# One denominator product for eight attention units inside the v projection, its rows folded by transfers

## Chip, cores, metric

One core of one Trainium2 chip. The metric is the device time of one execution in microseconds (us), as the median of several runs. Engines: PE is TensorE, DVE is VectorE, ACT is ScalarE, POOL is GpSimd, SP issues most DMAs. The kernel's tiles lie in SBUF, in up to 128 partitions; PE writes its products to PSUM tiles, from which ACT and DVE read them (for q: PE writes pq, ACT reads it as 128x512 and DVE as 128x1024). A record is one matmul in the trace.

## The reference, cut to what matters

Eight images of 512 channels by 1024 positions go through an attention block with eight heads, then a nonlocal block with a batch norm over all images.

```python
q = _conv1x1(x, Wq, bq).reshape(B, h, d, H * W)          # B 8, h 8, d 64, H*W 1024
k = _conv1x1(x, Wk, bk).reshape(B, h, d, H * W)
v = _conv1x1(x, Wv, bv).reshape(B, h, d, H * W)
attn = jax.nn.softmax(jnp.einsum('bhdn,bhdm->bhnm', q, k) * scale, axis=-1)
out = jnp.einsum('bhnm,bhdm->bhdn', attn, v).reshape(B, C, H, W)
return x + _conv1x1(out, Wp, bp)
```

The kernel sums the exponentials of each softmax row apart from the weighted sum, and multiplies o by the reciprocals of these denominators afterwards. That is all this change touches.

## The kernel before

The attention of an image is done in eight units (four pairs of heads, two halves of the queries). A unit's sums of exponentials end in `acc`, 128 partitions of 1024 columns. Four transfers turn each quarter of its partitions into 32 partitions of `fold`, so that four units fill one `fold` tile (a group), which three adds reduce to 128 x 1024. A matmul with a block matrix of ones (`folds`) sums each unit's 32 partitions: the denominators.

```python
def fold_parts(g, t, pin):
    return [lambda to=to, l=l, r=r: pin(nc.vector.tensor_tensor(to, l, r, ALU.add)) for to, l, r in (
        (t[:, 0], t[:, 0], t[:, 1]), (t[:, 2], t[:, 2], t[:, 3]), (folded[g][:, 0], t[:, 0], t[:, 2]))]

def denominators(g, ps):
    t = folded.pop(g)
    columns(ps, folds, lambda j: t[:, 0, j * 512:(j + 1) * 512])   # two matmuls, 64 columns each
    ...
    nc.vector.reciprocal(ri, ps)
    ...                                                            # ri goes to DRAM as den_d
    return d
# rows_of: two transfers a group spread den_d over 64 partitions each (r); normalize: o = o * r
```

In every image but the last, the first group is folded within the attention, the second in between the matmuls of the next image's q (`fills`). Both products stand between q and v:

```python
q, peak_q = heads_of(b + 1, "q", ..., fills=last_fold)
load_w(nc.sync)
d = [denominators(g, next_bank(f"den_{b}_{g}")[:, 0, :]) for g in range(2)]
v = values(b + 1, weights("WvT"), nxt["data"], {5: normalize(d)})   # products behind v's sixth chunk
```

The kernel uses PSUM as four tags of two banks each. A stage takes its tags from the list `free` in the order in which the stage before leaves them, and `next_bank` takes the tag that comes first and moves it to the end. A projection has up to seven chunks of matmuls, and each chunk's result is read from PSUM by ACT or DVE. `dve(...)` pins an instruction: it keeps its place in DVE's queue as written, where others are placed by a scheduler.

## Time and profile before

| | before |
|---|---|
| median of six runs | 2166.07 us (2164.36 to 2166.74) |
| span in the profile | 2164.2 us |
| PE busy | 2137.3 us, 99% of the span |
| DVE busy | 1427.6 us, 66% |
| waits of PE over 0.15 us | five, 5.6 us in all |

Read it from PE: its busy share and its few waits say that time is to be had only from matmuls that fall away and from those waits. The lines are in the prediction.

### The profile page before, as it was taken

Reading aid. Unit: us, or ns where it says so; the run is one execution under the profiler, and the core shown is the slowest. Engines: PE = TensorE matmul, PEld = TensorE weight load, DVE = VectorE, ACT = ScalarE, POOL = GpSimd, SP = SyncE. Lnnn points to the kernel's source line nnn. Section 1 sums busy time; section 2 is a strip of 40 time slices with the busy share of each in tenths; the row PEclk is TensorE's granted clock in tenths of the full one; section 3 lists DMA queues with packets and bytes.
Section 4 is the critical chain, followed back from the end, with each engine's and each line's share of the span. In section 5 each row is a group of like instructions: output and inputs, shape, how many; then the busy total and the mean of one; then the engine's idle time right before and its main releaser. Section 6 shows DMA issues by size and latency. Waiting matters only on the chain.

```text
span 2164.2 us, 29633 instructions
## 1 busy us (share of the span) xinstructions
PE 2137.3 (99%) x12454; PEld 1110.0 (51%) x12454; DVE 1427.6 (66%) x1612; ACT 740.9 (34%) x848; POOL 43.2 (2%) x50
## 2 busy tenths in 40 slices
PE   9999999999999999999999999999999999999996
PEld 4534664346733567335663366633665346643362
DVE  5477756776477764777747767477773776657736
ACT  1464104631046310563105621066212651056115
POOL 0000100000000000000000000000000000000000
PEclk9999999999999999999999999999999999999998
DMA  6312433123131232312323132231334114111748
GB/s 216 131 36 54 132 151 131 40 62 115 69 132 40 62 115 72 132 38 77 98 102 108 40 89 101 79 108 40 97 135 153 30 40 122 63 53 41 245 150 357
DMA packets 50701, 219.47 MB, mean 101 GB/s; under 512 B 9216, under 2 KB 15616, under 8 KB 43008
## 3 DMA queue, kind: packets, MB, share of 16 engines
q1 hardware_dynamic: 49072, 216.18, 31.2%
q8 instruction: 100, 1.64, 0.3%
q10 hardware_dynamic: 1488, 1.32, 0.2%
q14 instruction: 41, 0.34, 0.0%
HBM read 138.03 MB, written 45.88 MB: 85 GB/s over the span
## 4 chain that ended last, share of the span: by engine, by line
PE 98%; DVE 1%; ACT 1%; DMA 0%; issue 0%
PE ps L422 20%; PE po L448 20%; PE pv L274 9%; PE ptp L274 9%; PE pp L274 7%; PE pk L274 7%; PE pq L274 6%; PE pg L274 4%; PE pf L571 3%; PE pz L274 2%; PE pk_in_s L237 2%; PE pq_in_s L237 2%; PE pp_in_s L237 2%; PE pz L682 2%; PE pwf L606 1%; PE den L394 1%
## 5 line engine op out<-in xcount | busy, mean ns | idle before, releaser
L425 ACT ACTIVATE e<-ps 128x1024 f32<-128x1024 f32 x512 | 522.4, 1024 | 428.3 <-PE ps L422 422.1
L431 DVE TENSOR_TENSOR acc<-acc,e 128x1024 f32<-128x1024 f32 x384 | 470.0, 1224 | 127.7 <-ACT e L425 120.1
L448 PE MATMUL po<-e,v 64*64 64x512 f32 x4096 | 528.7, 589 | 0.7 <-ACT w_WgT L573 0.7
L422 PE MATMUL ps<-q,k 64*64 64x512 f32 x4096 | 529.1, 589 | 0.0
L448 PEld LDWEIGHTS po<-e,v 64*64 64x64 f32 x4096 | 156.5, 133 | 283.4 <-issue 275.4
L422 PEld LDWEIGHTS ps<-q,k 64*64 64x64 f32 x4096 | 155.6, 133 | 284.1 <-issue 275.0
L594 ACT ACTIVATE g<-pg,gb 128x512 f32<-128x512 f32 x31 | 21.3, 687 | 388.6 <-PE pg L274 385.7
L429 DVE TENSOR_TENSOR acc<-e,e 128x1024 f32<-128x1024 f32 x64 | 78.2, 1223 | 108.7 <-ACT e L425 73.4
L274 PE MATMUL ptp<-w_tp,t_x 128*128 128x256 f32 x512 | 115.0, 380 | 0.0
L274 PE MATMUL pv<-w_WvT,t_x 128*128 128x256 f32 x512 | 114.5, 379 | 0.0
L274 PEld LDWEIGHTS pv<-w_WvT,t_x 128*128 128x128 f32 x512 | 97.2, 190 | 13.2
L274 PEld LDWEIGHTS ptp<-w_tp,t_x 128*128 128x128 f32 x512 | 96.7, 190 | 12.9
L274 PE MATMUL pp<-t_o,w_WpT 128*128 128x512 f32 x208 | 100.8, 592 | 0.0
L274 PE MATMUL pq<-t_x,w_WqT 128*128 128x512 f32 x200 | 98.8, 593 | 0.7 <-DVE w_WqT L734 0.7
L274 PE MATMUL pk<-t_x,w_WkT 128*128 128x512 f32 x200 | 98.9, 592 | 0.0
L377 ACT COPY v<-pv 128x1024 f32<-128x1024 f32 x32 | 32.4, 1012 | 191.2 <-PE pv L274 191.2
L274 PE MATMUL pv<-w_WvT,x 128*128 128x256 f32 x384 | 87.5, 381 | 0.0
L274 PE MATMUL ptp<-w_tp,x 128*128 128x256 f32 x384 | 86.8, 379 | 0.0
L378 DVE TENSOR_TENSOR v<-v,pv 128x1024 f32<-128x1024 f32 x24 | 29.3, 1221 | 79.9 <-PE pv L274 79.9
L274 PEld LDWEIGHTS pv<-w_WvT,x 128*128 128x128 f32 x384 | 72.4, 190 | 15.7 <-issue 5.9
L274 PEld LDWEIGHTS ptp<-w_tp,x 128*128 128x128 f32 x384 | 73.0, 190 | 13.3 <-issue 3.6
L478 DVE TENSOR_TENSOR fold<-fold 128x1024 f32<-128x1024 f32 x48 | 58.7, 1222 | 26.0 <-DMA fold<-acc 25.5
(182 smaller groups left out, 2211.3 us busy)
## 6 DMA issues: line engine op xcount, KB each, us to landing
fold<-acc SPq DMA_DIRECT2D x254, 128.0 KB
r<-den_d SPq DMA_DIRECT2D x32, 512.0 KB
x<-in_x_dram SPq DMA_DIRECT2D x31, 512.0 KB
w_WqT<-kept_WqT SPq DMA_DIRECT2D x7, 2176.0 KB
w_WkT<-kept_WkT SPq DMA_DIRECT2D x7, 2176.0 KB
w_WpT<-kept_WpT SPq DMA_DIRECT2D x6, 2176.0 KB
w_WvT<-kept_WvT SPq DMA_DIRECT2D x7, 1792.0 KB
w_tp<-kept_tp SPq DMA_DIRECT2D x7, 1792.0 KB
```

What stands on the lines that cost most here:

```text
L237: pe(nc.tensor.matmul(ps, a[wi], d[di], start=s not in begun, stop=True, skip_group_check=True))
L274: pe(nc.tensor.matmul(to_ps, lhsT(k), rhs(k), start=(s, at) not in begun, stop=(k == nk - 1), skip_group_check=True))
L377: seven(f"pv_{b}", w, data, True, lambda q, ps: nc.scalar.copy(at(q), as_v(ps)), lambda q, ps: dve(nc.vector.tensor_tensor(at(q), at(q), a ...
L378: lambda q, ps: dve(nc.vector.tensor_tensor(at(q), at(q), as_v(ps), ALU.add)), between)
L422: pe(nc.tensor.matmul(ps[c * P // 2:(c + 1) * P // 2, j, :], k[r, p, keys], q[r, p, h * 512:(h + 1) * 512], start=True, stop=True, skip_gr ...
L425: nc.scalar.activation(e, ps, AF.Exp, scale=SCALE)
L429: nc.vector.tensor_tensor(accs[u], es[u, 0], e, ALU.add)
L431: ins = nc.vector.tensor_tensor(accs[u], accs[u], e, ALU.add)
L448: pe(nc.tensor.matmul(ps[j * D:(j + 1) * D, r, :], v[keys, m, (2 * p + j) * D:(2 * p + j + 1) * D], e[keys, j, :], start=(m == 0), stop=(m ...
L478: return [lambda to=to, l=l, r=r: pin(nc.vector.tensor_tensor(to, l, r, ALU.add)) for to, l, r in ((t[:, 0], t[:, 0], t[:, 1]), (t[:, 2], ...
L571: pe(nc.tensor.matmul(ps[:, c, :], tp[:, i, c * P:(c + 1) * P], tp[:, i, CI:], start=(i == 0), stop=(i == NB - 1)))
L682: pe(nc.tensor.matmul(ps[:, h - h0, :], wf[:, d, oc * P:(oc + 1) * P], g[d][:, h * 512:(h + 1) * 512], start=(d == 0), stop=(d == IC - 1), ...
```

## The change

Its intent: one product for all eight units of an image, so that PE does half the denominator work and DVE one reciprocal fewer. To put eight units on 128 partitions, each group's 32 rows per unit are folded to 16: two transfers per group bring the even rows to one place and the odd rows to another, and one more add sums them. The product moves behind v's first chunk, to give the transfers time. Apart from that, the last image's first reading of p is pinned behind the products of o with the rows.

```diff
-                    if done in (6, 8, 10) and fills:
-                        fills[done // 2 - 3]()
+                    if done in fills:
+                        fills[done]()
...
+        def fold_last():
+            t = folded.pop(1)
+            folded["all"] = t[:, 1]
+            adds = [lambda to=to, l=l, r=r: dve(nc.vector.tensor_tensor(to, l, r, ALU.add)) for to, l, r in (
+                (t[:, 0], t[:, 0], t[:, 1]), (t[:, 2], t[:, 2], t[:, 3]), (t[:, 0], t[:, 0], t[:, 2]),
+                (t[:, 1], t[:, 1], t[:, 3]))]
+            first = folded.pop(0)[:, 0]
+            def rows_of(g, half):
+                nc.sync.dma_start(t[g * D:(g + 1) * D, 1 + 2 * half, :],
+                                  (t[:, 0] if g else first).rearrange("(r s) n -> s r n", s=2)[half])
+            return {6: lambda: (adds[0](), rows_of(0, 0)), 8: lambda: (adds[1](), rows_of(0, 1)),
+                    10: lambda: (adds[2](), rows_of(1, 0), rows_of(1, 1)), 14: adds[3]}
...
+        def all_denominators(ps):
+            t = folded.pop("all")
+            columns(ps, folds8, lambda j: t[:, j * 512:(j + 1) * 512])
+            ...
...
+                if b == B - 1 and q == "11":
+                    dve(ins)
...
-            d = [denominators(g, next_bank(f"den_{b}_{g}")[:, 0, :]) for g in range(2)]
-            v = values(b + 1, weights("WvT"), nxt["data"], {5: normalize(d)})
+            def norm():
+                nxt["products"] = normalize(denominators(next_bank(f"den_{b}")[:, 0, :]))
+            v = values(b + 1, weights("WvT"), nxt["data"], {0: norm, 5: lambda: nxt["products"]()})
```

Cut: the building of `folds8` on POOL, the sharing of one tile by `warm` and `heads`, and the shape of `den_d`. The last image keeps two products.

More of the change, by code (lines that the diff above doesn't have):

```diff
@@ L300, in unshifted @@
     xt = xp.tile([P, CC, N], F32, tag="x", name="x_0")
-    warm = const.tile([P, P], F32, tag="warm", name="warm")
-    nc.vector.memset(warm, 0.0)
+    heads = const.tile([P, P], F32, tag="heads", name="heads")
+    nc.vector.memset(heads, 0.0)
     _, w_first = weights_tile("WqT", C // 2)
@@ L315, in unshifted @@
     for i in range(WARM):
-        pe(nc.tensor.matmul(ps[:, :P], warm, warm, start=True, stop=True))
+        pe(nc.tensor.matmul(ps[:, :P], heads, heads, start=True, stop=True))
     bq, bk = load_col("bq", nc.scalar), load_col("bk", nc.scalar)
@@ L328, in unshifted @@
         nc.vector.memset(folds[i * P // 4:(i + 1) * P // 4, i * D // 4:(i + 1) * D // 4], 1.0)
-    heads = const.tile([P, P], F32, tag="heads", name="heads")
-    nc.vector.memset(heads, 0.0)
+    folds8 = const.tile([P, D], F32, tag="folds8", name="folds8")
+    nc.gpsimd.memset(folds8, 0.0)
+    nc.gpsimd.affine_select(out=folds8, in_=folds8, compare_op=ALU.is_gt, fill=1.0, base=1 - P // 8,
+                            pattern=[[-P // 8, 8], [0, D // 8]], channel_multiplier=1)
+    nc.gpsimd.affine_select(out=folds8, in_=folds8, compare_op=ALU.is_ge, fill=0.0, base=0,
+                            pattern=[[-P // 8, 8], [0, D // 8]], channel_multiplier=1)
     for j in range(2):
@@ L479, in fold_parts @@
                 (t[:, 0], t[:, 0], t[:, 1]), (t[:, 2], t[:, 2], t[:, 3]), (folded[g][:, 0], t[:, 0], t[:, 2]))]
+        def all_denominators(ps):
+            t = folded.pop("all")
+            columns(ps, folds8, lambda j: t[:, j * 512:(j + 1) * 512])
+            ri = t[:, :512]
+            nc.vector.reciprocal(ri, ps)
+            d = dram2.tile([16, 512], F32, tag="den", name=f"den_d_{b}")
+            nc.sync.dma_start(d, ri.rearrange("(a s) n -> a s n", a=16)[:, 0, :])
+            d = d.rearrange("(j g i) n -> g j (i n)", j=2, g=2)
+            return d[0], d[1]
         def denominators(g, ps):
@@ L491, in denominators @@
             nc.sync.dma_start(d, ri.rearrange("(a s) n -> a s n", a=8)[:, 0, :])
-            return d
+            return d.rearrange("(j i) n -> j (i n)", j=2)
         def rows_of(g, d):
@@ L498, in rows_of @@
             for j in range(2):
-                sp(nc.sync.dma_start(rows[g][j * D:(j + 1) * D, :],
-                                     d.rearrange("(j i) n -> j (i n)", j=2)[j].partition_broadcast(D)))
+                sp(nc.sync.dma_start(rows[g][j * D:(j + 1) * D, :], d[j].partition_broadcast(D)))
         def normalize(d):
@@ L530, in attention @@
             return o["o"], lambda ps: denominators(1, ps), lambda d: normalize((first_den, d)), None
-        return o["o"], denominators, normalize, fold_parts(1, folded[1], dve)
+        return o["o"], all_denominators, normalize, fold_last()
     def project(b, xt, o, w, between, data=None):
@@ L539, in first @@
                 at = xt[:, c, cols(q)]
-                nc.vector.scalar_tensor_tensor(at, ps[:, m, :], bp[:, c:c + 1], at, ALU.add, ALU.add)
+                ins = nc.vector.scalar_tensor_tensor(at, ps[:, m, :], bp[:, c:c + 1], at, ALU.add, ALU.add)
+                if b == B - 1 and q == "11":
+                    dve(ins)
         seven(f"pp_{b}", w, data or data_sums(quarters_of(o), f"o_{b}"), False, first, add_to(xt), between,
```

## The prediction

> **What bounds the kernel now.** I read the page first, the totals and the chain that ended last:
>
> ```profile
> PE 2137.3 (99%) x12454; PEld 1110.0 (51%) x12454; DVE 1427.6 (66%) x1612; ACT 740.9 (34%) x848; POOL 43.2 (2%) x50
> ...
> PE 98%; DVE 1%; ACT 1%; DMA 0%; issue 0%
> ```
>
> TensorE (PE) is busy 99% of the span and makes 98% of the chain, so the time falls only by matmuls that are not issued, or by PE's idle time. How much idle time there is to win, the waits of PE alone tell:
>
> ```profile
> PE pp L274 <- DVE o L513: 2.6, 1, 2.6
> PE warm_ps L316 <- DVE warm L302: 1.1, 1, 1.1
> PE pq L274 <- DVE w_WqT L734: 0.7, 1, 0.7
> PE po L448 <- ACT w_WgT L573: 0.7, 1, 0.7
> PE den L394 <- PE pg L274: 0.5, 1, 0.5
> ```
>
> Five waits, 5.6 us, only one of them large. Work taken from VectorE (DVE, 66% busy) or from the DMA queues is worth nothing by itself.
>
> Next, the timeline of PE where image 3 hands over to image 4 (other images repeat it), the place of the denominators:
>
> ```profile
> 1007.99 1.88 PE L274 MATMUL pq<-t_x,w_WqT 128*128 128x512 f32 x4
> 1009.80 1.94 PE L394 MATMUL den<-fold,folds 128*64 128x512 f32 x8
> 1011.67 3.72 PE L274 MATMUL pv<-w_WvT,x 128*128 128x256 f32 x16
> ```
>
> Two groups of denominators (four units each) stand one after the other between q and v. PE gives them 1011.67 - 1009.80 = 1.87 us. In the last image a group stands alone, in the timeline there:
>
> ```profile
> 1977.46 1.08 PE L394 MATMUL den<-fold,folds 128*64 128x512 f32 x4
> 1978.47 1.09 PE L422 MATMUL ps<-q,k 64*64 64x512 f32 x8
> ```
>
> One group costs 1978.47 - 1977.46 = 1.01 us, so the second of two costs 1.87 - 1.01 = 0.86 us. (The source issues two matmuls a group and the trace shows four records: each f32 product counts as two.)
>
> What DVE does at that hand-over (its timeline, image 3):
>
> ```profile
> 1005.95 1.21 DVE L296 TENSOR_TENSOR q<-q,pq 128x1024 f32<-128x1024 f32 x1
> 1007.08 0.41 DVE L296 TENSOR_TENSOR q<-q,pq_in_s 128x256 f32<-128x256 f32 x1
> 1007.41 2.34 DVE L363 TENSOR_REDUCE peak_q<-q 128x1 f32<-128x1024 f32 x2
> 1009.91 2.35 DVE L296 TENSOR_TENSOR q<-q,pq 128x1024 f32<-128x1024 f32 x2 [0.16 <-PE pq L274]
> 1012.18 3.35 DVE L487 RECIPROCAL fold<-den 128x512 f32<-128x512 f32 x1
> ```
>
> From 1005.6 to 1021 DVE has no idle time over 0.2 us: q's last partial sums are read from PSUM at 1009.91 to 1012.26, and 3.35 us reciprocals follow.
>
> Last, the one large wait, in the timeline of the last image:
>
> ```profile
> 2025.15 1.10 SPq L499 DMA_DIRECT2D r<-den_d  x2
> 2025.19 2.36 DVE L513 TENSOR_TENSOR o<-o,r 128x1024 f32<-128x1024 f32 x2 [0.90 <-DMA r<-den_d]
> ...
> 2030.27 3.60 PE L274 MATMUL pp<-o,w_WpT 128*128 128x512 f32 x8
> 2033.90 1.41 DVE L540 SCALAR_TENSOR_TENSOR x<-pp,bp,x 128x512 f32<-128x512 f32 x2 [5.09 <-PE pp L274]
> 2035.23 2.35 DVE L513 TENSOR_TENSOR o<-o,r 128x1024 f32<-128x1024 f32 x2
> 2036.50 5.40 PE L274 MATMUL pp<-o,w_WpT 128*128 128x512 f32 x8 [2.63 <-DVE o L513]
> ```
>
> DVE idles 5.09 us, reads the first products of p, and only then multiplies the second half of o by the reciprocals' rows, for which PE waits 2.63 us. DVE is a queue in order, and the reading, which waits for PE, stands ahead of the products.
>
> [...] the last image's first two rows transfers were issued at 2018.25 in bars of 1.11 us together, and the product that needs them waited until 2025.19, 6.94 us after. So when data is there must be read from the waiters.
>
> **The change, part by part** (images 0 to 6 are ordinary; the last keeps its own way, two separate groups).
>
> (a) One product for eight units. Per ordinary image it removes one group of den on PE (0.86 us, on the path: PE never stops there), one reciprocal (3.35 us of DVE) and one write of den to DRAM. It adds four transfers of 256 KB and one add of 1.22 us. On PE: 7 x 0.86 = 6.0 us. On DVE: 7 x (3.35 - 1.22) = 15 us fewer, worth nothing in time.
>
> (b) The product moves from before v to after v's first chunk. A chunk of v is 16 records, 3.45 us by the starts of chunks. The folding has to be done by then. In image 3 the three adds of the second group end at about 1002.2; the transfers of its rows start there. Four transfers of 128 KB from acc to fold in the last image fed their first add 3.4 us after the first issue (issued 2009.41, add at 2012.82); 512 KB again here, so I estimate landing at 1006 to 1007. The closing add stands behind the adds at 1007.08, starts at about 1007.5 and ends at 1008.7. PE comes to den at 1009.80 + 3.45 = 1013.25. So the transfers are hidden.
>
> But the same 1.22 us pushes what DVE does next: peak_q ends at 1011.0 instead of 1009.75, q's last two sums at about 1013.3 instead of 1012.26. By the rotation of PSUM banks in the source, the new den takes the very bank that q's last chunk used (the spare one of v), so it must wait for those sums: 1013.3 plus a tenth for the signal, against 1013.25. I charge 0.1 us an image, 0.7 us in all.
>
> After den: its reciprocal ends by 1019 (with a peak_q of 2.28 ahead of it), the write and the rows follow, issued at about 1021, where before it was 1023 (second reciprocal ended 1021.0). Rows in use start at the product behind v's sixth chunk, some 1 us earlier than now. They are as early as before or earlier: no new wait.
>
> (c) The pinned first reading of the last p. The second pair of rows was issued at 2025.15; with the same 6.94 us as the first pair they are there at 2032.1. The two products then run 2032.1 to 2034.5, the one PE needs first ends at 2033.3, before PE has finished p's first chunk (about 2033.87, 2.63 us before 2036.50). PE's wait of 2.63 us goes whole. The reading starts at 2034.5 instead of 2033.9; its bank is used again two chunks after the next, near 2040.7, so nothing waits for it. The end follows: behind this point PE has no wait over 0.15 us to its last matmul at 2143.5, and the outputs, written at the pace of DMA from the first finished channel group on, start earlier by the same amount.
>
> (d) warm becomes heads, and folds8 is built on GpSimd at the start: heads' ones wait for the warm-up matmuls, which end near 4.9 us, while DVE's next work comes at 8.27. Nothing.
>
> Sum: -6.0 - 2.6 + 0.7 = -7.9 us; 2166.1 - 7.9 = 2158.2, so I say **2158**.
>
> **The rivals.** First, the bank: q's last sums come later than I think (the add waits for the rows' transfers, or the scheduler puts the second peak_q, 2.28 us, ahead of them), and den holds PE each time. For it: DVE is packed there, and the margin is nil. Against it: the sums are pinned in order and ready at 1009.9. At 1 us an image it costs 7 us: some 2164. Second, the rows come too late for the products and DVE, in order, holds v's sums and p or k: for it, four transfers of 512 KB take about 2.4 us each; against it, DVE loses a whole reciprocal ahead of them. With 0.5 us an image: 2161. Third, no bank wait at all: -8.6 us, 2157.4. Fourth, (c) gains little, because the second pair of rows shares the DMA engines with the weights and spills issued behind it and lands after 2033.9: then 2159 to 2160.
>
> **Range and chances.** Runs of the kernel before lie within 2.3 us. The third rival sets the near edge, with that scatter 2155; the others, partly, the far one, 2162. 2% is 43 us: nothing here reaches it either way.
>
> **What would show it.** Right: den has 36 records instead of 64, standing behind the first 16 records of pv; reciprocals 9 instead of 16; from q's last to k's first matmul 0.86 us less in every ordinary image; the wait of pp for o gone and no idle time of DVE between rows and reading; a new entry "den waits for DVE q" of a tenth of a us, seven times. Wrong: that entry at half a us or more, a wait of DVE's o for r in ordinary images with PE gaps behind it in pv or pk, adds of fold waiting for transfers, or pp still waiting.

## The result, and the profile after

| | before | after |
|---|---|---|
| median of six runs | 2166.07 us | 2172.98 us (2169.47 to 2174.78) |
| span in the profile | 2164.2 us | 2173.1 us |

The ratio is 1.0031, 95% interval 1.0018 to 1.0044. (Ratios are the mean time of one kernel's fast runs over that of the other's in the same rounds, so not quite the ratio of the medians quoted.) The change cost 6.9 us where 7.9 us of gain were predicted. It stays within 2%, but outside the range.

The page of the kernel after, busy times and chain:

```profile
PE 2135.7 (98%) x12426; PEld 1110.9 (51%) x12426; DVE 1412.5 (65%) x1611; ACT 741.5 (34%) x848; POOL 44.0 (2%) x53
...
PE 97%; issue 1%; DVE 1%; ACT 1%; DMA 0%
```

The 28 records (7 images x 4) are gone, and DVE has 15 us less to do, as reckoned. But PE's busy time fell by 1.6 us only, and "issue", time for which no releaser is found, is now 1% of the chain. The waits of PE in the kernel after (columns: total us, times, longest):

```profile
PE den L398 <- issue: 13.4, 7, 2.0
PE warm_ps L316 <- DVE heads L302: 1.1, 1, 1.1
PE po L452 <- ACT w_WgT L605: 0.7, 1, 0.7
PE den L398 <- PE pg L274: 0.4, 1, 0.4
```

The wait of pp for o is gone. In its place PE waits before each of the seven new products, up to 2.0 us. The profile names no releaser: PE's sequencer, not DVE or a DMA, stands as the last thing seen. What happens there is shown by the timeline of the hand-over, image 3 of the kernel after (PE, DVE and ACT together; starts are 6.94 us later than in the kernel before, by the last four records of q, 1014.93 against 1007.99):

```profile
1014.93 1.88 PE L274 MATMUL pq<-t_x,w_WqT 128*128 128x512 f32 x4
...
1016.07 1.23 DVE L485 TENSOR_TENSOR fold<-fold 128x1024 f32<-128x1024 f32 x1 [1.64 <-DMA fold<-fold]
1016.64 3.62 PE L274 MATMUL pv<-w_WvT,x 128*128 128x256 f32 x16
...
1017.21 2.34 DVE L367 TENSOR_REDUCE peak_q<-q 128x1 f32<-128x1024 f32 x2
1019.46 2.34 DVE L296 TENSOR_TENSOR q<-q,pq 128x1024 f32<-128x1024 f32 x2
...
1021.91 1.08 PE L398 MATMUL den<-fold,folds 128*64 128x512 f32 x4 [1.65 <-issue]
1022.92 1.35 PE L274 MATMUL pv<-w_WvT,t_x 128*128 128x256 f32 x5
```

Follow DVE down: it idles 1.64 us until the rows have been transferred, adds them, reduces peak_q, and only then reads q's last sums from PSUM, until 1021.80. PE has done v's first chunk at 1020.26, waits 1.65 us, and starts den 0.1 us after q's sums have been read. DVE's wait and PE's wait have the same length, and over the seven images too: DVE waits 13.3 us for these transfers, PE 13.4 us for den. The closing add itself was done at 1017.3. So it is not den's input that holds it.

There is a second loss. The granted clock of PE in three stretches around image 6's den (columns: stretch, us, busy us and count of PE, PEld, DVE, ACT, POOL, then PE's clock, DMA share, GB/s):

```profile
1806.90:1808.90 2.00, 0.01 (x2) 0.04 (x2) 1.97 (x3) 1.00 (x1) 0.00 (x0) 1.00 1.07 453
1808.90:1812.80 3.90, 3.90 (x10) 2.24 (x11) 3.90 (x3) 0.00 (x0) 0.00 (x0) 0.57 0.35 147
1812.80:1816.00 3.20, 3.20 (x16) 2.81 (x16) 1.63 (x1) 0.70 (x1) 0.00 (x0) 0.99 0.04 10
```

PE stands still for 2 us, then runs 3.9 us at a mean clock of 0.57. The records of the clock hold three windows of 3.41 us at 0.5 within the work: after the waits of 1.99, 2.04 and 2.04 us (images 0, 1, 6), none after those of 1.65 to 1.95 us. Each costs 3.41 / 2 = 1.7 us: in image 0 the 32 records of pv behind den take 8.83 us, in image 4, without a window, 7.17 us.

The windows begin at 218.83, 488.48 and 1809.44, 0.55 to 0.98 us after den has started, so the half clock falls on the matmuls behind the wait. Why 1.99 us brought one and 1.95 us did not, these runs do not settle.

The last image, where the pinning acts (timeline of the kernel after):

```profile
2038.43 1.10 SPq L530 DMA_DIRECT2D r<-den_d  x2
2038.47 2.36 DVE L543 TENSOR_TENSOR o<-o,r 128x1024 f32<-128x1024 f32 x2 [1.31 <-DMA r<-den_d]
...
2043.13 7.29 PE L274 MATMUL pp<-o,w_WpT 128*128 128x512 f32 x16
2045.44 2.36 DVE L543 TENSOR_TENSOR o<-o,r 128x1024 f32<-128x1024 f32 x2 [3.35 <-DMA r<-den_d]
```

The second pair of products now starts when its rows land, 7.01 us after their issue (6.94 was assumed), and pp runs through. In the kernel before, the wait of 2.63 us was followed by a half-clock window too (3.41 us from 2036.64 on): eight records of pp took 5.40 us there, and 16 take 7.29 us here.

Adding up by the profiles, from one hand-over to the next: images with no window lose 0.85 to 1.16 us (image 2 to 3: 266.33 against 265.31), those with one 2.85 to 2.90 us (image 0 to 1: 269.87 against 267.02). Together +12.8 us. From the last image's second den to PE's last matmul: 122.01 us against 126.34, -4.3 us. With 0.3 us at the two ends of the program that makes the 8.8 us between the spans (the profiled run was the slowest of the six).

### The profile page after: what moved, and what is told of

Its sections match the earlier page's. It is cut to its first block, busy times and chain, and to the rows that moved or that the text cites.

```text
span 2173.1 us, 29636 instructions
## 1 busy us (share of the span) xinstructions
PE 2135.7 (98%) x12426; PEld 1110.9 (51%) x12426; DVE 1412.5 (65%) x1611; ACT 741.5 (34%) x848; POOL 44.0 (2%) x53
## 4 chain that ended last, share of the span: by engine, by line
PE 97%; issue 1%; DVE 1%; ACT 1%; DMA 0%
PE ps L426 20%; PE po L452 20%; PE pv L274 9%; PE ptp L274 9%; PE pp L274 7%; PE pk L274 7%; PE pq L274 6%; PE pg L274 4%; PE pf L603 3%; PE pz L274 2%; PE pk_in_s L237 2%; PE pq_in_s L237 2%; PE pp_in_s L237 2%; PE pz L714 2%; PE pwf L638 1%
## 5 line engine op out<-in xcount | busy, mean ns | idle before, releaser
L274 PE MATMUL pv<-w_WvT,t_x 128*128 128x256 f32 x512 | 119.5, 391 | 0.0
L274 PEld LDWEIGHTS ptp<-w_tp,x 128*128 128x128 f32 x384 | 73.0, 190 | 13.3 <-issue 3.6
L274 PEld LDWEIGHTS pv<-w_WvT,x 128*128 128x128 f32 x384 | 73.0, 190 | 13.3 <-issue 3.6
L393 POOL TENSOR_SCALAR q<-q,gates 128x1024 f32<-128x1024 f32 x32 | 35.2, 1119 | 1673.3 <-DVE gates L391 1673.3
```

Of the source, the lines that this page charges most:

```text
L274: pe(nc.tensor.matmul(to_ps, lhsT(k), rhs(k), start=(s, at) not in begun, stop=(k == nk - 1), skip_group_check=True))
L393: nc.gpsimd.tensor_scalar(q[:, p, :], q[:, p, :], gate[:, p:p + 1], 1.0, ALU.mult, ALU.mult)
```

## The experiments

Theory: den stands in the PSUM bank of q's last chunk; late row transfers hold DVE; DVE therefore reads that bank late; PE waits, and a wait near 2 us can bring a window at half clock. Rivals: den waits for its input, whatever its bank; DVE is too full even with transfers in time; the windows are chance.

Three kernels are wrong (e3, e6, e8). The comparison with the reference passed them all the same, so passing it says little about denominators here. The other kernels are right by construction.

### e1_pin_only: the kernel before and the pinning alone

```diff
-                nc.vector.scalar_tensor_tensor(at, ps[:, m, :], ...)
+                ins = nc.vector.scalar_tensor_tensor(at, ps[:, m, :], ...)
+                if b == B - 1 and q == "11":
+                    dve(ins)
```

> The kernel before with only the pinned first reading of the last p. What it is worth is disputed. The prediction charged the wait of PE alone: 2.63 us, so 2163.5. Reading the two traces side by side, the records of the granted clock show one window of 3.41 us at half clock at 2036.6 in the kernel before, just at that wait, and none there after the change; pp's eight records took 5.40 us there instead of 3.6. If the wait brings that window, its going is worth 2.63 + 3.41/2 = 4.3 us: 2161.8, with PE's wait for o gone and no half-clock window between 2030 and 2045.

Measured: 2162.14 us against 2165.46 (nine runs of the kernel before on the same chip), ratio 0.9985, interval 0.9971 to 0.9998. No window between 2030 and 2045. PE's timeline there:

```profile
2029.94 7.13 PE L274 MATMUL pp<-o,w_WpT 128*128 128x512 f32 x16
2036.90 7.03 PE L274 MATMUL pp<-t_o,w_WpT 128*128 128x512 f32 x16
```

No wait and full speed. The median gained 3.3 us, between the two values, and the runs of the kernel before fit an explanation: five with a mean granted clock of 0.996 took 2164.5 to 2165.5 us, four with 0.995 took 2165.9 to 2166.9. So the pinning is worth some 2.6 us in every run and 1.7 us more in those where the wait brought its window. The profiled run of before was one of these; the others were not profiled, and only their mean clock speaks for it.

### e2_other_bank: den in a bank that nobody reads

```diff
-                nxt["products"] = normalize(denominators(next_bank(f"den_{b}")[:, 0, :]))
+                nxt["products"] = normalize(denominators(bank(free[2], f"den_{b}")[:, 0, :]))
```

> The changed kernel with one line altered: den takes the PSUM bank that v uses only from its sixth chunk on, instead of the spare bank, in which q's last sums still stand. The order of instructions is the same on every engine. Bank theory: PE's waits before den (1.65 to 2.04 us in seven images, 13.4 us) are waits for q's last sums to be read; they go, with them the three half-clock windows; 7 x 0.86 = 6.0 us and the 4.3 us of the pinned reading remain: about 2156 (2155 to 2157). Rival, inputs theory: den waits for the closing add of the rows, whatever its bank; then waits of about 1.5 to 2 us stay and the time stays near 2171 to 2175. The trace of the changed kernel favours the bank: the closing add ends 2.9 us before PE is through v's first chunk.

Measured: 2155.69 us (2155.61 to 2155.95) against 2165.46, ratio 0.9955, interval 0.9941 to 0.9969. PE has no wait before the seven dens, and the half-clock windows are gone. Image 3 of this kernel, two answers of the timeline (DVE, then PE):

```profile
1006.34 1.23 DVE L485 TENSOR_TENSOR fold<-fold 128x1024 f32<-128x1024 f32 x1 [1.59 <-DMA fold<-fold]
...
1009.74 2.34 DVE L296 TENSOR_TENSOR q<-q,pq 128x1024 f32<-128x1024 f32 x2
```

```profile
1006.97 3.62 PE L274 MATMUL pv<-w_WvT,x 128*128 128x256 f32 x16
1010.51 1.08 PE L398 MATMUL den<-fold,folds 128*64 128x512 f32 x4
```

DVE waits for the transfers just as long as in the changed kernel (1.59 us, 13.2 us in all), and q's sums end at 1012.08. But den starts at 1010.51, right behind the chunk. The instructions stand in the same order on every engine; only banks differ (den's, and through the list `free` those of the stages behind v). That shows the bank as what PE waited for, and the input theory falls. It is also the version that beats both kernels, with one line.

### e3_no_row_wait: the closing add without its transfers (wrong)

```diff
-            folded["all"] = t[:, 1]
+            folded["all"] = t[:, 2]
...
-                (t[:, 1], t[:, 1], t[:, 3]))]
+                (t[:, 2], t[:, 2], t[:, 0]))]
```

> The changed kernel, wrong results on purpose: the closing add takes data that needs no transfer, and den reads its result; the four transfers of rows still run, nobody reads them. Order on the engines unchanged. Late-transfer theory: DVE's wait for the rows (1.6 to 2.0 us an image) is what pushes q's last sums beyond the end of v's first chunk; without it they end near 1020.3 on the changed kernel's scale, so den waits 0 to 0.4 us, no half-clock windows, about 2157 (2156 to 2159). Rival, full-queue theory: the added 1.22 us and the peak_q of 2.34 us ahead of the sums are enough by themselves; then den still waits 1 us or more in each image: 2163 or more.

Measured: 2156.46 us (2155.77 to 2157.17), ratio 0.9959. No wait before den. Image 3, two answers of the timeline (DVE, then PE):

```profile
1008.40 2.34 DVE L296 TENSOR_TENSOR q<-q,pq 128x1024 f32<-128x1024 f32 x2
```

```profile
1007.31 3.62 PE L274 MATMUL pv<-w_WvT,x 128*128 128x256 f32 x16
1010.86 1.08 PE L398 MATMUL den<-fold,folds 128*64 128x512 f32 x4
```

q's sums had been read at 1010.74 and den started at 1010.86, where the chunk ended: the margin is nil, as the prediction had it, but enough. So the full-queue theory falls: with the rows in time, the changed kernel would have been right as it was written.

### e6_rows_side_by_side: neighbouring partitions as the source (wrong)

```diff
-  (t[:, 0] if g else first).rearrange("(r s) n -> s r n", s=2)[half])
+  (t[:, 0] if g else first).rearrange("(s r) n -> s r n", s=2)[half])
```

> The changed kernel, wrong results on purpose: each of the four transfers of rows takes 64 neighbouring partitions as its source instead of every second one. Same size, count, order, destinations. Why do they take 1.95 us each (256 KB, last landing 6.9 us after the first adds are done) where I had reckoned with 512 KB in 3.4 us? Stride theory: every second partition as the source; side by side they land in 1.3 us or less each, the last some 2 us earlier, DVE's wait for them goes and the time falls to about 2157 to 2160. Rival, destination theory: 64 partitions as the destination set the pace; then landing spacing stays 1.9 to 2.0 us, DVE still waits 1.6 to 2.0 us, and the time stays 2169 to 2175.

Measured: 2155.73 us (2155.5 to 2155.9), ratio 0.9954. The row of the transfers in the DMA view (last column: median us from issue to landing), the changed kernel and then e6:

```profile
fold<-fold SPq DMA_DIRECT2D x28, 256.0 KB, 4.8
```

```profile
fold<-fold SPq DMA_DIRECT2D x28, 256.0 KB, 3.0
```

The same bytes to the same 64 partitions land in 3.0 us instead of 4.8. Successive landings stand 1.9 us apart in the changed kernel and some 1.3 us here, where the first gaps are those of the issues (1.5 and 1.3 us in image 3). The first of the four, with none of them ahead of it, lands in 4.2 to 4.4 us there and in 2.9 to 3.0 us here, so the queue is not all of it. The destination alone does not set the pace.

### e8_rows_spread: every second partition on both sides (wrong on purpose, one look)

```diff
-                nc.sync.dma_start(t[g * D:(g + 1) * D, 1 + 2 * half, :],
+                nc.sync.dma_start(t[:, 1 + 2 * half, :].rearrange("(r s) n -> s r n", s=2)[g],
```

> The changed kernel, wrong results on purpose: the transfers of rows take every second partition as in the change, but write to every second partition as well instead of 64 neighbouring ones. Side-by-side source and destination landed in 3.0 us (median, issue to landing) against 4.8 us for the change. Stride theory (a stepped source is slow by itself): stays at 4.5 to 5 us, PE still waits for den. Mismatch theory (128 partitions spread over on one side, 64 on the other, is what is slow): 3.5 us or less, and no wait of PE before den.

```profile
fold<-fold SPq DMA_DIRECT2D x28, 256.0 KB, 2.3
```

Measured: 2156.06 us (a single run, state unknown), landing in 2.3 us, faster than side by side. So a stepped source is not slow by itself: what is slow here, with 4.8 us, is to read from partitions spread over all 128 and to write to 64 neighbouring ones. The gaps between landings say the same: the fourth transfer, issued 0.5 to 0.6 us behind the third, lands 1.15 us behind it in e6 and 0.63 us in e8, against 1.9 us in the changed kernel (image 3; 256 KB, so an estimate of some 230 GB/s for 64 to 64, some 420 for spread to spread and 138 for the mixed case). The mixed case is slower than either matched one, and no run here shows its cause.

### e10_spread_right: the same with a right result

The edit of e8, and `folds8` built for the new places (even partitions hold units 0 to 3, odd ones 4 to 7):

```diff
...
+    for g in range(2):
+        for i in range(4):
+            r = slice(i * P // 4, (i + 1) * P // 4)
+            nc.vector.tensor_copy(folds8[r, g * P // 4 + i * 8:g * P // 4 + (i + 1) * 8],
+                                  parity[r, g:g + 1].to_broadcast([P // 4, 8]))
...
```

> The changed kernel with source and destination of the four transfers of rows both on every second partition, and the matrix of the den product rebuilt so that the result is right (even rows hold the first four units, odd rows the others). Bank and place of den as changed. The mismatch theory, shown by one look at a wrong kernel, should hold for a right one: transfers land in 2.3 us (median) instead of 4.8, DVE does not wait for them, q's last sums are read in time, PE does not wait for den: about 2156, as fast as with the other bank and no faster, since PE then has nothing left to win here. Rival: it was luck of the one look, and waits of 1 us and more remain: 2165 or more.

Measured: 2155.77 us (2154.96 to 2156.09) against 2165.75, ratio 0.9955, interval 0.9942 to 0.9969; landing in 2.3 us, DVE waits for no rows, PE for no den. A second cure, at the other end of the chain, as good as e2 and no better.

### e5_den_second and e7_den_third: the product later in v

```diff
-            v = values(..., {0: norm, 5: lambda: nxt["products"]()})
+            v = values(..., {1: norm, 5: lambda: nxt["products"]()})      # e5; 2: norm in e7
```

> The changed kernel with the one product of denominators behind v's second chunk instead of its first; bank and everything else as changed. PE then asks for den's bank 3.45 us later, after q's last sums have been read (they ended 1.65 to 2.04 us after v's first chunk). Bank theory: no wait of PE before den, no half-clock windows, 2155.7 as with the other bank. Rows theory (a reciprocal started later brings the rows too late, DVE stands in front of the products and holds v's or k's sums): the reciprocal starts only some 0.7 us later than with the other bank, where the last pair of rows landed 1.8 us before its product, so it should not show; if it does, PE waits in pk and 2157 or more.

> The same, behind v's third chunk: 3.45 us later again. Looks for the other edge of the window. The last pair of rows should land about 2 us after DVE comes to its products, so DVE waits for r some 2 us in each of seven images. Rows theory: part of it reaches PE in pk, 0.3 to 1 us an image, 2158 to 2163. Rival: DVE has room there, PE does not notice: 2155.7 with DVE's wait for r plainly there.

Measured: e5 2156.01 us (ratio 0.9957, interval 0.9941 to 0.9974), no wait before den: a third cure, the bank and the transfers left as they were. e7 2157.45 us (2157.31 to 2157.75), ratio 0.9965. In e7, DVE waits 12.5 us for r in nine places, where e5 has 5.0 us in two: 1.1 us an image, half of what I expected. PE loses 1.4 us against e5 in all; the profile of e7 has 1.1 us of that as a wait at the very start of the program (other kernels show 0 to 1.0 us there), so what the late rows cost PE is not settled, but it is small.

### e9_longer_gap: what a wait does to the clock

```diff
-                    10: ..., 14: adds[3]}
+                    10: ..., 14: lambda: (adds[3](), *(dve(nc.vector.tensor_tensor(t[:, i], t[:, i], t[:, i], ALU.add))
+                                                      for i in (3, 2, 0)))}
```

> The changed kernel with three more adds of 1.22 us on DVE behind the closing add, before q's last sums (one peak_q of 1.17 us falls behind the sums instead): PE's waits before den grow by about 2.3 us to some 4 us. In the changed kernel's profile waits of 1.99, 2.04 and 2.04 us were each followed by 3.41 us at half clock and those of 1.65 to 1.95 us were not. Clock theory: waits this long all bring one: seven half-clock windows, time 2155.7 + 7 x (4 + 1.7) = about 2196 (2192 to 2199). Rival, chance theory (the windows come in some share of the images whatever the wait): about three windows, 2155.7 + 7 x 4 + 3 x 1.7 = about 2189 or less.

Measured: 2200.6 us (2200.12 to 2201.3), ratio 1.0164. Waits of 4.16 to 4.36 us before den, 29.7 us in all, and all seven images have half-clock time: three windows of 3.41 us and four of 6.83 us. PE in image 0 of this kernel:

```profile
220.16 1.97 PE L398 MATMUL den<-fold,folds 128*64 128x512 f32 x4 [4.31 <-issue]
222.06 8.72 PE L274 MATMUL pv<-w_WvT,t_x 128*128 128x256 f32 x32
```

The four records of den take 1.97 us here instead of 1.08 and the next 32 of pv 8.72 us instead of 7.17 (in e2). The mean granted clock of the profiled run is 0.987, against 0.996 in e2. The chance theory falls for waits this long: half-clock time followed all seven. What makes it one window or two, these runs do not settle. My 2196 was 4 us short because I had not thought of double windows: PE is busy for 15.5 us more than in e2, where seven single windows make 11.9, and the waits came to 29.7 us instead of 28.

### e11_after_again: the changed kernel, a second profile

> The changed kernel once more, unaltered, for its scatter and a second profile. If the half-clock windows follow PE's waits of about 2 us in some images only, then runs spread over 2169 (no window: 2155.7 + 13.4) to 2176, and in the profile each window of 3.41 us stands right after one of the longer waits before den and adds some 1.7 us to that image. Rival: the spread is of another origin; then the fast and slow runs have the same mean granted clock.

Measured: 2172.76 us (2170.40 to 2174.39). Waits of 2.02, 1.98 and 2.04 us in images 0, 1 and 6, each followed by a window; waits of 1.59 to 1.90 us in the other four, and none there. The same three images have windows in both profiles, so the second is no independent proof of what brings them. Of its four runs, the slowest (2174.39) had a clock of 0.993, the others (2170.40 to 2172.77) 0.995; in the first set of six, 2174.78 had 0.993 and the fastest, 2169.47, had 0.996. So the scatter fits the windows: 2155.7 us without waits (e2) + 13.4 of waits = 2169.1 with no window, + 3 x 1.7 = 2174.2 with three.

## Why the prediction was wrong

The chain that bounds the kernel and the parts' own costs were right; one term of part (b) was not.

- **(a) One group of den fewer: right.** PE spends 1.01 us on den in an ordinary image (1021.91 to 1022.92) instead of 1.87. The sum of this is in e2 against e1: 2162.14 - 2155.69 = 6.4 us, 6.0 predicted; the starts of the two programs differ by some tenths.
- **(b) "So the transfers are hidden": this step failed.** I estimated landing at 1006 to 1007 us from transfers acc to fold, which go from 32 partitions to 32 neighbouring ones. The last rows landed at 1016.04, which is 1009.1 on the scale of the kernel before, since the new transfers go from every second partition to 64 neighbouring ones, land in 4.8 us and follow each other at 1.9 us. In e6, with 64 neighbouring partitions on both sides, the last rows landed at 1004.07, 1006.4 on the same scale: the estimate would have held for such transfers. The closing add started 1.6 us later than predicted (1009.1 instead of 1007.5), and all that stands behind it in DVE's queue, q's last sums included, was as late. **"I charge 0.1 us an image, 0.7 us in all"** is the mis-sized term: it measured 1.65 to 2.04 us an image, 13.4 us in all.
- **The bank: right as a mechanism.** That den takes the bank of q's last chunk, and that the margin is nil, was said; e2 shows the first and e3 the second. The first rival, in the words "the add waits for the rows' transfers", was what happened. I gave it 1 us an image and let it into the range only partly, although no trace had measured this kind of transfer and the margin was nil. Even taken in whole it says 2164, not 2173: the waits were nearly twice as long, and the windows came on top. Two of the signs of being wrong that the prediction names came true, waits of half a us or more before den and adds of fold that wait for transfers; the view calls the waits "issue", not "DVE q".
- **The clock: not seen.** Neither the term nor the rivals counted that a wait of PE can bring 3.41 us at half clock. It cost up to 5.1 us here (three windows). The timeline that the prediction quotes held the hint: eight records of pp took 5.40 us behind the wait of 2.63 us.
- **(c) The pinning: right, and worth more than reckoned.** 2.6 us, and 1.7 us more in the runs where the wait had brought a window; the rows landed in time, 7.01 us after issue. The fourth rival fell.
- **Rows too late for the products** (second rival): did not happen; with the product at its place DVE waits for r only in the last image. **(d)** cost nothing that the profiles show.

Sum for the profiled run: -6.0 (den) + 13.4 (waits) + 5.1 (windows) - 4.3 (the last p with its window) = +8.2 us, against 8.8 measured between the spans. Of the other 0.6 us, 0.3 stand at the two ends of the program; the rest is not accounted for.

## What to carry to other kernels

When work is moved, ask of its PSUM bank who read it last, and through which queue that reader has to come: a wait in an in-order queue (here DVE for a transfer) passed one to one to an engine that has nothing to do with it (DVE waited 13.3 us, PE 13.4 us), because there was no margin between them. Where the margin is nil, choose another buffer or a later place first; both cost one line here and turned a loss of 6.9 us into a gain of 9.8 us over the kernel before (e2). Take the time of a transfer only from one with the same spread of partitions on both sides: 256 KB landed in 4.8 us (median) from every second partition to 64 neighbouring ones, in 3.0 us from 64 neighbouring to 64 neighbouring, and in 2.3 us from every second to every second. And count a wait of PE near 2 us or more together with the half-clock window that may follow it: in the two profiles of the changed kernel and the one of the kernel before, 3.41 us at half clock followed all seven waits of 1.98 to 2.63 us and none of the eight of 1.59 to 1.95 us.
